# Remaining-row products of the feed-forward layer moved beside attention, with Silu built from Exp

## The chip, the cores and the metric

The kernel runs on one core of a Trainium2 chip, in fp32. The metric is device time in microseconds; the engines are TensorE (PE; its weight loads are PEld), VectorE (DVE), ScalarE (ACT), GpSimd (POOL) and SyncE (SP), whose queue issues most DMAs.

## The reference

One transformer block with modulation by a condition vector c, for x of 2 batches x 1024 tokens x 1024 features (`attn`, `ffn` abridged):

```python
mod = (silu(c) @ wmod).reshape(2, 6, 1, -1)          # sa, ca, ga, sb, cb, gb
h = layernorm(x) * (1 + ca) + sa
q, k, v = split(clip(h @ Wqkv.T, -8, 8))              # q, k: LayerNorm over 1024
scores = q k^T * 32**-0.5 + slope * (key - query)     # 32 heads of 32, causal
x = x + ga * (softmax(scores) @ v) @ Wout.T           # ga bounded away from 0
h = layernorm(x) * (1 + cb) + sb
act = silu((h @ Wg.T) * ag) * ((h @ Wu.T) * au)       # 2752 inner rows
x = x + gb * ((act @ Wd.T) * ad)
```

## The kernel before, in words

**Products.** Large products use a scheme of seven block products in place of eight (`seven`, the list `SEVEN`): a token block of 256 and a 1024-wide weight are split in 2 x 2 blocks, sums of blocks (A11, S1, ..., T1, ...) are multiplied, and the partial products P1, P2, U2, P5, U3, P53, U6 gather in two PSUM banks (`banks.pair()`). A partial product kept for later (P1, U2, P5) is copied out by ScalarE, its mate is added by VectorE.

**The inner rows.** Of the 2752 inner rows of the feed-forward layer, 2560 are handled in five groups by such products in the late stages. The last 192 (`REST`: 128 and 64 rows, here the *remaining rows*) are multiplied plainly: for each batch b and token block j (four of 256 tokens each) three *pieces* of eight matmuls, 128x256, over K = 1024: gate of 128 rows, up of 128 rows, and gate and up of 64 rows in one. Silu of the gate times the up goes to `rest_dram` for the down product.

**Stages in order.** (1) Modulation and projections of batch 0. (2) Attention of both batches: `attention` yields after each piece of work of a *unit* (four heads, one key block of 128), and `together` lays a generator of dense work, `dense_work`, between: projections of batch 1 while batch 0's attention runs, output products of batch 0 and of the first half of batch 1 while batch 1's runs. How much dense work is laid in by a given point follows from planned costs: `share(a)` with LEAD, DENSE0 and DENSE1, in planned us; a pair of 512-wide products counts 1.8. PE runs in exactly the order written (`pinned`); the other engines' and SP's order is set by a scheduler. (3) A stage of its own: the output products of batch 1's blocks j = 2, 3, all remaining-row products, and `second_batch`, which forms differences of the two batches' h2. (4) Gate and up products (gx, gy, ux, uy), with POOL forming weight sums. (5) Down products.

**A unit of attention.** Scores of four heads (two PSUM tiles sc0, sc1, one buffer each), Exp on ScalarE into p, a causal select on POOL, two units later the product with v (av), and sums of p on VectorE or POOL (`adders`). At the end of a group `settle` sums p over keys (`ones`) through a *turn bank* and stores it; after a group of 512 queries `reciprocals` loads the sums, inverts them and stores them.

**The output of one block**, `output`: `operand` loads the reciprocals (`rb`, four broadcasting DMAs) and ao, multiplies them and forms A11, A12, A21, A22, S1, S2, S4. 28 products follow; `read` adds mates, multiplies by the gate ga and adds to the residual rows xr. x1 is stored, rows are normalized to xn (`normalize`: bn_stats on VectorE, Ln and Exp on ScalarE, a correction on VectorE), and four transposes per block with scale and shift to h2 (`turned`, into h2t) are put on a list, `Todo`. `Todo.run` takes from this list between the products of the next block, each entry with the next turn bank (`banks.turn()`). In batch 1's attention there is a single turn bank, shared with `settle`.

**Buffers.** xr has four, A21 and A22 two each, A11, A12 and the S sums one. The remaining rows' weights are loaded after attention on ScalarE's queue, into memory of the attention pools; h2 blocks come back from memory by `fetch` (hl). Four PSUM banks (rps) hold their results.

Of the kernel before, what the change touches and what calls it, by code (L numbers as in the profile page):

```python
# [12 lines left out]
FP = mybir.dt.float32  # L13
AF = mybir.ActivationFunctionType
ALU = mybir.AluOpType
# [465 lines left out]
def kernel(  # L481
# [262 lines left out]
    def matmul(*args, **kw_):  # L744
        return in_order(nc.tensor.matmul(*args, **kw_))  # L745
# [112 lines left out]
    class Todo:  # L858
# [8 lines left out]
        def run(self, n, all_=False):  # L867
            for _ in range(min(n, len(self.list))):
                if not all_ and not self.banks.fresh():
                    return  # L870
                self.list.pop(0)(self.banks.turn())
                yield TURN

        def places(self, q0, n, side=lambda e: None):

# [337 lines left out]
    def operand(b, j, ap_):  # L1213

        qb, y0 = 2 * j * P // QB, 2 * j * P % QB
        rb = ap_.tile([P, KC, 2 * P], FP, tag="rb", name=f"rb_{b}_{j}")
        for g in range(4):
            nc.sync.dma_start(
                rb[ts(g, HD)],
                rec_dram[b][qb].rearrange("(k g) q -> g k q", g=4)[g][:, ds(y0, 2 * P)].partition_broadcast(HD),  # L1220
            )
        a = {
            q: ap_.tile(
                [P, KC // 2, P], FP, tag=q, name=f"ao{q}_{b}_{j}",
                bufs=2 if q in ("A21", "A22") else None,
            )
            for q in ("A11", "A12", "A21", "A22", "S1", "S2", "S4")
        }
        for m, kh, q, eng in (
            (0, 0, "A11", nc.vector), (0, 1, "A12", nc.gpsimd), (1, 1, "A22", nc.vector), (1, 0, "A21", nc.gpsimd),  # L1230
        ):
            nc.sync.dma_start(a[q], ao_dram[b][qb][:, ds(kh * 4, 4), ds(y0 + m * P, P)])
            eng.tensor_mul(a[q], a[q], rb[:, ds(kh * 4, 4), ts(m, P)])
        nc.vector.tensor_add(a["S1"], a["A21"], a["A22"])
        nc.vector.tensor_sub(a["S2"], a["S1"], a["A11"])
        a["S3"] = a["A21"]
        nc.gpsimd.tensor_sub(a["S3"], a["A11"], a["A21"])
        nc.gpsimd.tensor_sub(a["S4"], a["A12"], a["S2"])
        return a

    gates = {}

    def output(b, js, pools, banks, bt, todo, keep, made={}, q0=1):

        gap_, ap_, tkp, partp, hbp, sm = pools
        while (b, 2 * js[0] * P // QB) not in settled:
# [6 lines left out]
        for j in js:  # L1253
# [11 lines left out]
            def read(q, bank):  # L1265
                if q in ("P1", "U2", "P5"):
                    part_t[q] = partp.tile([P, 512], FP, tag=q, name=f"o{q}_{b}_{j}")
                    nc.scalar.copy(part_t[q], bank)
                    return
                m, n = QUAD[q]  # L1270
                yg = partp.tile([P, 512], FP, tag=f"yg{n}", name=f"yg_{q}_{b}_{j}")
                if q == "U6":
                    nc.vector.tensor_mul(yg, ga[:, ts(n, HALF)], bank)
                else:
                    nc.vector.tensor_add(yg, part_t[MATE[q]], bank)
                    nc.gpsimd.tensor_mul(yg, yg, ga[:, ts(n, HALF)])
                nc.gpsimd.tensor_add(xs[m][:, ts(n, HALF)], xs[m][:, ts(n, HALF)], yg)

# [10 lines left out]
            for m in range(2):  # L1289
                for g in range(2):  # L1290
                    def go(bank, m=m, g=g, xn=xn, h2=h2, j=j):
                        turned(
                            xn[m], bank, lambda k: h2[:, k, m, :],
                            lambda k: modt[:, 4, k, b : b + 1], lambda k: modt[:, 3, k, b : b + 1], g, False,
                        )
                        if (m, g) == (1, 1):
                            nc.sync.dma_start(h2_dram[b][j], h2)
                            if b == 0:
                                inner_b("B11", h2[:, 0 : KC // 2], j, hbp, nc.vector)
                                inner_b("B21", h2[:, KC // 2 :], j, hbp, nc.vector)  # L1300
                    todo.add(go)

    def second_batch(j, pool, h0, h1):

# [16 lines left out]


    OUT_US = 112.0
    LEAD, DENSE0, DENSE1 = 16.0, 370.0, 136.0

    def halves(half, jb):
        return (nc.vector, nc.gpsimd)[half]
# [14 lines left out]
            eng.dma_start(dst, src_[:, ds(r, n)].rearrange("(k p) f -> p k f", p=P))  # L1342
        return w

    def rest_rows(pairs, rest_w, pool, psp, tiles):

        n1 = REST[1][1]
        ib = 4 * NSB
        for b, j in pairs:
            hl = tiles[b, j].rearrange("p k h t -> p k (h t)")  # L1350
            ps = []
            for r in range(3):
                bank = psp.tile([P, 512], FP, tag="rp", name=f"rest_{b}_{j}_{r}")[:, 0:256]
                for k in range(KC):
                    matmul(bank, rest_w[r][:, k, :], hl[:, k, :], start=(k == 0), stop=(k == KC - 1))
                ps.append(bank)
                yield 3.4
            sg = pool.tile([P, 2, 256], FP, tag="rsg", name=f"rsg_{b}_{j}")
            ac = pool.tile([P, 2, 256], FP, tag="rac", name=f"rac_{b}_{j}")
            nc.scalar.activation(sg[:, 0], ps[0], AF.Silu, scale=vt[:, R_AG + ib : R_AG + ib + 1])  # L1360
            nc.scalar.activation(
                sg[64 : 64 + n1, 1], ps[2][0:n1], AF.Silu, scale=vt[0:n1, R_AG + ib + 1 : R_AG + ib + 2]
            )
            nc.vector.scalar_tensor_tensor(
                ac[:, 0], ps[1], vt[:, R_AU + ib : R_AU + ib + 1], sg[:, 0], ALU.mult, ALU.mult
            )
            nc.vector.scalar_tensor_tensor(
                ac[64 : 64 + n1, 1], ps[2][64 : 64 + n1],
                vt[64 : 64 + n1, R_AU + ib + 1 : R_AU + ib + 2], sg[64 : 64 + n1, 1], ALU.mult, ALU.mult,
            )  # L1370
            nc.sync.dma_start(rest_dram[0][:, b, j], ac[:, 0].rearrange("p (h t) -> p h t", h=2))
            nc.sync.dma_start(
                rest_dram[1][0:n1, b, j], ac[64 : 64 + n1, 1].rearrange("p (h t) -> p h t", h=2)
            )

    def in_range(pool, psp):

# [90 lines left out]
    def dense_work():  # L1468
        yield from dense0
        with tc.tile_pool(name="wdsum", bufs=2) as dwp:  # L1470
            steps = itertools.chain.from_iterable(down_weights(i, dwp) for i in range(4 * NSB))

            def side(n, e):
                at = 7 * n + e
                if at % 2 == 0 and at >= 2:
                    next(steps, None)

            yield from projections(1, qpools, banks, 1, side=side)
            for _ in steps:
                pass  # L1480
        early.close()
        hbp = right["hb"] = ost.enter_context(tc.tile_pool(name="hb", bufs=1))
        wop = ost.enter_context(tc.tile_pool(name="wo", bufs=1))
        gap_, tkp, partp, osm, aop = [
            ost.enter_context(tc.tile_pool(name=n, bufs=k))
            for n, k in (("oga", 1), ("tok", 4), ("opart", 1), ("osmall", 2), ("ao", 1))
        ]
        opools = (gap_, aop, tkp, partp, hbp, osm)
        made = {(0, 0): operand(0, 0, opools[1])}
        bt = weights_b(wop, wout_t, "o", wt_dram[3])  # L1490
        out_args.extend((opools, banks, bt, Todo(banks), keep))
        yield from output(0, range(NJ), *out_args, made)
        yield from output(1, range(NJ // 2), *out_args)

# [10 lines left out]

    together(attention(apools, (halves, mostly), banks), dense_work(), share)
    att.close()
    opools, _, bt, todo, _ = out_args
    pair_st = ctx.enter_context(ExitStack())
    rest_st = ctx.enter_context(ExitStack())  # L1510
    pair_pool = right["rest"] = pair_st.enter_context(tc.tile_pool(name="pair", bufs=1, side="right"))
    rest_pool = rest_st.enter_context(tc.tile_pool(name="rest", bufs=1, side="right"))
    rps = rest_st.enter_context(tc.tile_pool(name="rest_ps", bufs=4, space=PSUM))

    def fetch(b, j, eng=nc.sync):
        kept[b, j] = pair_pool.tile(
# [1 line left out]
        )  # L1518
        eng.dma_start(kept[b, j], h2_dram[b][j])

    def rows(*pairs):
        return rest_rows(pairs, rest_w, rest_pool, rps, kept)

    def second(j):
        for go in sum(second_batch(j, pair_pool, kept[0, j], kept[1, j]), []):
# [1 line left out]

    def with_turns(rows_):

        together(rows_, todo.run(len(todo.list), True), lambda a: 0.16 * (a - 9.0))  # L1530

    fetch(0, 0, nc.scalar)
    rest_w = rest_weights(rest_pool, nc.scalar)
    fetch(1, 0, nc.scalar)
    made = {(1, NJ // 2): operand(1, NJ // 2, opools[1])}
    fetch(0, 1)
    with_turns(rows((0, 0), (1, 0)))
    fetch(1, 1)

    def between():  # L1540
        yield from rows((0, 1))
        second(0)
        yield from rows((1, 1))

    together(
        between(), output(1, range(NJ // 2, NJ), *out_args, made, 3), lambda a: 0.6 * OUT_US / 2 * a / 20.6
    )
    in_range(rest_pool, rps)
    fetch(0, 2)
    second(1)  # L1550
    fetch(0, 3)
    with_turns(rows((0, 2), (1, 2)))
    second(2)
    alone(rows((0, 3), (1, 3)))
    ost.close()
    late_pools.close()
    pinned[0] = False
# [438 lines left out]
```

## Time and profile before

| | us |
|---|---|
| median of 3 runs (lowest, highest) | 2951.07 (2949.82, 2956.16) |
| the profiled execution | 2953.39 |
| its span, first to last instruction | 2951.7 |
| mean granted TensorE clock, share of full speed | 0.971 |

One profiled execution gives all lines of this document. In a timeline row the columns are start, duration, engine, source line, operation, output and input, shape and count, and in brackets the idle time before it and what ended it. A group row gives minimum, median and maximum in ns. A row of stages gives for each engine its busy time and, in brackets, its instructions. A fp32 matmul is two instructions in the trace.

### The profile page before, as it was taken

To read this page: it belongs to the slowest core of one execution; us is meant where nothing else is said; L and a number is where in the kernel's file an instruction comes from. 1 tells how busy PE (TensorE), PEld (TensorE's weight loads), DVE (VectorE), ACT (ScalarE), POOL (GpSimd) and SP (SyncE) were. 2 spreads that over 40 slices of the span, in tenths; PEclk is the share of its full clock that TensorE was granted. 3 is DMA by queue.
4 is the path that set the end of the run, shared out by engine and by line. 5 is a ranking of instruction groups with operands and counts; after the bars stand their busy time and mean duration, and the time that the engine had idled before them with its cause. 6 is when DMAs were issued, how large, how long until landed. Compare 5 with 4: busy or idle time off the path is not lost. (4 is left out here: it accounts for less than half of the span.)

```text
span 2951.7 us, 29883 instructions
## 1 busy us (share of the span) xinstructions
PE 2733.9 (93%) x10271; PEld 1338.6 (45%) x10271; DVE 1434.9 (49%) x2285; ACT 686.6 (23%) x1523; POOL 1289.9 (44%) x1270
## 2 busy tenths in 40 slices
PE   6999897899999898878798999999999998999998
PEld 2444332333333232222465444444444446888776
DVE  5666522456553454655554344453535445434442
ACT  1222232354434455555111011010101100000000
POOL 3312145524363665556357346463644641222343
PEclk9999998999999889999899999999999999999999
DMA  8777787462652644432676758575765759554542
GB/s 335 296 256 283 295 287 229 140 221 92 221 164 69 216 151 144 148 106 85 184 239 216 245 174 283 162 269 178 243 213 176 245 156 283 162 157 135 164 146 80
DMA packets 377571, 579.12 MB, mean 196 GB/s; under 512 B 21590, under 2 KB 278712, under 8 KB 366276
## 3 DMA queue, kind: packets, MB, share of 16 engines
q1 hardware_dynamic: 359768, 554.54, 58.0%
q10 hardware_dynamic: 17644, 22.59, 2.5%
q8 instruction: 84, 1.38, 0.2%
q14 instruction: 75, 0.61, 0.1%
HBM read 411.89 MB, written 165.17 MB: 196 GB/s over the span
## 5 line engine op out<-in xcount | busy, mean ns | idle before, releaser
L1056 ACT ACTIVATE p<-sc,kw 128x128 f32<-128x128 f32 (+3 forms) x1024 | 422.2, 514 | 353.9 <-PE sc L745 340.7
L745 PE MATMUL bank<-wT,a 128*128 128x512 f32 x768 | 364.7, 619 | 14.0 <-DVE raw L951 7.1
L1088 POOL TENSOR_TENSOR p<-p,p 128x1024 f32<-128x1024 f32 (+3 forms) x128 | 264.1, 2064 | 236.5 <-PE av L745 209.3
L1088 DVE TENSOR_TENSOR p<-p,p 128x1024 f32<-128x1024 f32 (+3 forms) x192 | 239.7, 1261 | 187.9 <-POOL p L1060 141.4
L745 PE MATMUL bank<-wB,a 128*128 128x512 f32 x576 | 264.3, 603 | 3.2 <-DVE raw L951 1.9
L745 PE MATMUL sc<-cq,ck 32*128 32x512 f32 (+3 forms) x1536 | 196.3, 553 | 69.9 <-ACT p L1056 69.7
L745 PEld LDWEIGHTS bank<-wT,a 128*128 128x128 f32 x768 | 144.0, 197 | 202.6 <-issue 183.9
L1060 POOL TENSOR_SCALAR_AFFINE_SELECT p<-p 128x256 f32<-128x256 f32 x256 | 135.6, 543 | 148.1 <-ACT p L1056 146.0
L745 PE MATMUL av<-p,cv 128*32 128x512 f32 (+3 forms) x1536 | 174.0, 517 | 19.2 <-POOL p L1060 19.2
L745 PEld LDWEIGHTS bank<-wB,a 128*128 128x128 f32 x576 | 104.6, 190 | 149.1 <-issue 129.7
L745 PEld LDWEIGHTS sc<-cq,ck 32*128 32x128 f32 x1536 | 66.1, 190 | 201.3 <-ACT p L1056 121.2
L1781 PE MATMUL gy<-bt,sig 128*128 128x512 f32 x280 | 133.5, 599 | 12.2 <-DMA bt<-bop_B 8.3
L1781 PE MATMUL uy<-bt,siu 128*128 128x512 f32 x280 | 132.2, 594 | 0.0
L1781 PE MATMUL ux<-bt,siu 128*128 128x512 f32 x280 | 131.6, 592 | 0.0
L1781 PE MATMUL gx<-bt,sig 128*128 128x512 f32 x280 | 131.6, 592 | 0.0
L745 PEld LDWEIGHTS av<-p,cv 128*32 128x32 f32 x1536 | 33.8, 110 | 137.4 <-issue 85.5
L951 DVE TENSOR_TENSOR raw<-P,bank 128x512 f32<-128x512 f32 x48 | 32.9, 685 | 126.8 <-PE bank L745 117.5
L1781 PEld LDWEIGHTS gy<-bt,sig 128*128 128x128 f32 x280 | 52.6, 190 | 82.5 <-issue 74.1
L1781 PEld LDWEIGHTS uy<-bt,siu 128*128 128x128 f32 x280 | 53.6, 192 | 67.8 <-issue 66.6
L1781 PEld LDWEIGHTS gx<-bt,sig 128*128 128x128 f32 x280 | 53.2, 190 | 67.0 <-issue 66.6
L1781 PEld LDWEIGHTS ux<-bt,siu 128*128 128x128 f32 x280 | 53.2, 190 | 67.0 <-issue 65.1
L745 PE MATMUL rest<-hl,restw 128*128 128x256 f32 x288 | 67.7, 394 | 14.9 <-DMA restw<-in_L_ffn_Wu_dram 14.9
(416 smaller groups left out, 4510.7 us busy)
## 6 DMA issues: line engine op xcount, KB each, us to landing
bt<-bop_T SPq DMA_DIRECT2D x140, 512.0 KB
bt<-bop_B SPq DMA_DIRECT2D x99, 512.0 KB
a<-hop SPq DMA_DIRECT2D x20, 1792.0 KB
wm<-in_L_wmod_dram SPq DMA_DIRECT2D x48, 512.0 KB
wB<-in_L_attn_Wqkv_dram SPq DMA_DIRECT2D x21, 1024.0 KB
aq_S<-act_S SPq DMA_DIRECT2D x16, 1280.0 KB
qk<-qs SPq DMA_DIRECT2D x16, 1024.0 KB
act_S<-asS SPq DMA_DIRECT2D x30, 512.0 KB
```

The costliest lines, as they stand in the source:

```text
L745: return in_order(nc.tensor.matmul(*args, **kw_))
L951: nc.vector.tensor_add(dst, part_t[MATE[q]], bank)
L1056: nc.scalar.activation(p[:, g, lo:hi], sp[:, g, lo:hi], AF.Exp, bias=kw[:, d, h_ : h_ + 1])
L1060: nc.gpsimd.affine_select(out=p[:, :, 0:P], in_=p[:, :, 0:P], pattern=[[0, 2], [1, P]], compare_op=ALU.is_ge, fill=0.0, base=0, channel_mu ...
L1088: adders[b](half, jb).tensor_add(dst, dst, ps[half][:, :, 0:n])
L1781: nc.tensor.matmul(ps.rearrange("p (j t) -> p j t", j=NJ), ins[mat][qa][:, c2, :], bt[:, :, c2, :], start=(q in ("P1", "P2", "P5") and c2 ...
```

## The change

`rest_rows` becomes `rest_piece`: one piece is an entry of the `Todo` list, behind the four transposes of its block, and works on the block's h2 still on chip. So the pieces of batch 0 and of batch 1's blocks 0 and 1 are taken between output products. Blocks 2 and 3 of batch 1 stay after the output. The weights are loaded on SP's queue with the pools of the output stage; DENSE1 goes from 136 to 205 planned us. Silu(g) is formed as g / (1 + exp(-g)): Identity and Exp on ScalarE, then a minimum with an addition, a reciprocal and a product on VectorE. To make room xr gets two buffers, A21 and A22 one, and the gated partial sum is formed in place of its own tile. After attention the list is emptied, with two more turn banks, then the output of blocks 2 and 3 of batch 1 runs by itself.

```diff
-                self.list.pop(0)(self.banks.turn())
-                yield TURN
+                more = self.list.pop(0)(self.banks.turn())
+                if more is None:
+                    yield TURN
+                else:
+                    yield from more
...
-                bufs=2 if q in ("A21", "A22") else None,
...
-                yg = partp.tile([P, 512], FP, tag=f"yg{n}", name=f"yg_{q}_{b}_{j}")
                 if q == "U6":
+                    yg = partp.tile([P, 512], FP, tag="yg", name=f"yg_{q}_{b}_{j}")
                     nc.vector.tensor_mul(yg, ga[:, ts(n, HALF)], bank)
                 else:
-                    nc.vector.tensor_add(yg, part_t[MATE[q]], bank)
+                    yg = part_t[MATE[q]]
+                    nc.vector.tensor_add(yg, yg, bank)
...
+            if rest is not None:
+                for r in range(3):
+                    todo.add(rest_piece(b, j, r, *rest))
...
-    LEAD, DENSE0, DENSE1 = 16.0, 370.0, 136.0
+    LEAD, DENSE0, DENSE1 = 16.0, 370.0, 205.0
...
+    def rest_piece(b, j, r, rest_w, pool):
...
+        def go(bank):
+            hl = kept[b, j].rearrange("p k h t -> p k (h t)")
+            ps = bank[:, 0:256]
+            for k in range(KC):
+                matmul(ps, rest_w[r][:, k, :], hl[:, k, :], start=(k == 0), stop=(k == KC - 1))
+            if r != 1:
+
+                g, e = tile_("rg", r), tile_("re", r)
+                nc.scalar.activation(g[hi], ps[lo], AF.Identity, scale=ag_)
+                nc.scalar.activation(e[hi], g[hi], AF.Exp, scale=-1.0)
+                nc.vector.tensor_scalar(e[hi], e[hi], FAR, 1.0, ALU.min, ALU.add)
+                nc.vector.reciprocal(e[hi], e[hi])
+                nc.vector.tensor_mul(g[hi], g[hi], e[hi])
+                sig[b, j, gate] = g
+            if r != 0:
+                ac = tile_("rac", r)
+                nc.vector.scalar_tensor_tensor(ac[hi], ps[hi], au_, sig[b, j, gate][hi], ALU.mult, ALU.mult)
+                nc.sync.dma_start(
...
+            yield 3.5
...
-            for n, k in (("oga", 1), ("tok", 4), ("opart", 1), ("osmall", 2), ("ao", 1))
+            for n, k in (("oga", 1), ("tok", 2), ("opart", 1), ("osmall", 2), ("ao", 1))
         ]
+        rwp = ost.enter_context(tc.tile_pool(name="restw", bufs=1))
...
-    rps = rest_st.enter_context(tc.tile_pool(name="rest_ps", bufs=4, space=PSUM))
+    rps = rest_st.enter_context(tc.tile_pool(name="rest_ps", bufs=2, space=PSUM))
...
-        together(rows_, todo.run(len(todo.list), True), lambda a: 0.16 * (a - 9.0))
-
-    fetch(0, 0, nc.scalar)
-    rest_w = rest_weights(rest_pool, nc.scalar)
-    fetch(1, 0, nc.scalar)
+        together(rows_, todo.run(len(todo.list), True), lambda a: 0.3 * (a - 3.0))
+
+    banks.others = banks.others + [rps.tile([P, 512], FP, tag=f"rq{i}", name=f"rq{i}", bufs=1) for i in range(2)]
     made = {(1, NJ // 2): operand(1, NJ // 2, opools[1])}
+    fetch(0, 0)
+    fetch(1, 0)
+    alone(todo.run(len(todo.list), True))
     fetch(0, 1)
-    with_turns(rows((0, 0), (1, 0)))
     fetch(1, 1)
-
-    def between():
-        yield from rows((0, 1))
-        second(0)
-        yield from rows((1, 1))
-
-    together(
-        between(), output(1, range(NJ // 2, NJ), *out_args, made, 3), lambda a: 0.6 * OUT_US / 2 * a / 20.6
-    )
+    second(0)
+    alone(output(1, range(NJ // 2, NJ), *out_args[:-1], None, made, 3))
     in_range(rest_pool, rps)
+    second(1)
     fetch(0, 2)
-    second(1)
     fetch(0, 3)
-    with_turns(rows((0, 2), (1, 2)))
+    with_turns(rows(2))
     second(2)
-    alone(rows((0, 3), (1, 3)))
+    alone(rows(3))
```

More of the change, by code (lines that the diff above doesn't have):

```diff
@@ L1241, with output @@
     gates = {}
-    def output(b, js, pools, banks, bt, todo, keep, made={}, q0=1):
+    def output(b, js, pools, banks, bt, todo, keep, rest=None, made={}, q0=1):
         gap_, ap_, tkp, partp, hbp, sm = pools
@@ L1343, in rest_weights @@
         return w
-    def rest_rows(pairs, rest_w, pool, psp, tiles):
+    def rest_piece(b, j, r, rest_w, pool):
         n1 = REST[1][1]
         ib = 4 * NSB
[L1349 to L1362, printed above, removed]
-            )
[L1364 to L1374, printed above, removed]
@@ new lines, in rest_piece, with tile_ @@
+        gate, lo = (0, slice(0, P)) if r < 2 else (1, slice(0, n1))
+        hi = slice(64, 64 + n1) if gate else lo
+        ag_, au_ = (vt[rows_, R_ + ib + gate : R_ + ib + gate + 1] for rows_, R_ in ((lo, R_AG), (hi, R_AU)))
+        def tile_(nm, r):
+            return pool.tile([P, 256], FP, tag=nm, name=f"{nm}_{b}_{j}_{r}")
+        def go(bank):
[15 more added lines that the diff above has]
+                nc.sync.dma_start(
+                    rest_dram[gate][0 : n1 if gate else P, b, j], ac[hi].rearrange("p (h t) -> p h t", h=2)
+                )
+            yield 3.5
@@ L1376, in in_range @@
+        return go
+    sig = {}
     def in_range(pool, psp):
@@ L1490, in dense_work @@
         bt = weights_b(wop, wout_t, "o", wt_dram[3])
-        out_args.extend((opools, banks, bt, Todo(banks), keep))
+        rest = rest_weights(rwp, nc.sync), rwp
+        out_args.extend((opools, banks, bt, Todo(banks), keep, rest))
         yield from output(0, range(NJ), *out_args, made)
@@ L1507 @@
     att.close()
-    opools, _, bt, todo, _ = out_args
+    opools, _, bt, todo, _, rest = out_args
     pair_st = ctx.enter_context(ExitStack())
@@ L1519, in fetch, with rows @@
         eng.dma_start(kept[b, j], h2_dram[b][j])
-    def rows(*pairs):
-        return rest_rows(pairs, rest_w, rest_pool, rps, kept)
+    def rows(j):
+        for r in range(3):
+            yield from rest_piece(1, j, r, *rest)(rps.tile([P, 512], FP, tag="rp", name=f"rest_{j}_{r}"))
     def second(j):
@@ L1528, in with_turns @@
     def with_turns(rows_):
-        together(rows_, todo.run(len(todo.list), True), lambda a: 0.16 * (a - 9.0))
-    fetch(0, 0, nc.scalar)
-    rest_w = rest_weights(rest_pool, nc.scalar)
-    fetch(1, 0, nc.scalar)
+        together(rows_, todo.run(len(todo.list), True), lambda a: 0.3 * (a - 3.0))
+    banks.others = banks.others + [rps.tile([P, 512], FP, tag=f"rq{i}", name=f"rq{i}", bufs=1) for i in range(2)]
     made = {(1, NJ // 2): operand(1, NJ // 2, opools[1])}
+    fetch(0, 0)
+    fetch(1, 0)
+    alone(todo.run(len(todo.list), True))
     fetch(0, 1)
-    with_turns(rows((0, 0), (1, 0)))
     fetch(1, 1)
-    def between():
-        yield from rows((0, 1))
-        second(0)
-        yield from rows((1, 1))
-    together(
-        between(), output(1, range(NJ // 2, NJ), *out_args, made, 3), lambda a: 0.6 * OUT_US / 2 * a / 20.6
-    )
+    second(0)
+    alone(output(1, range(NJ // 2, NJ), *out_args[:-1], None, made, 3))
     in_range(rest_pool, rps)
+    second(1)
     fetch(0, 2)
-    second(1)
     fetch(0, 3)
-    with_turns(rows((0, 2), (1, 2)))
+    with_turns(rows(2))
     second(2)
-    alone(rows((0, 3), (1, 3)))
+    alone(rows(3))
     ost.close()
```

## The prediction

> **What bounds the kernel now.** I read the page's busy line first, then the stages, since one share over 2951.7 us says little. TensorE (PE) is busy 93%, so time comes only from stretches where it waits, or from work laid into them. The profile in stages:
>
> ```profile
> PE 2733.9 (93%) x10271; PEld 1338.6 (45%) x10271; DVE 1434.9 (49%) x2285; ACT 686.6 (23%) x1523; POOL 1289.9 (44%) x1270
> ```
> ```profile
> core 0: us, PE busy (x) PEld busy (x) DVE busy (x) ACT busy (x) POOL busy (x), PEclk, DMA share, GB/s
> 390.00:990.00 600.00, 555.69 (x2522) 204.68 (x2520) 279.43 (x431) 238.96 (x559) 281.42 (x279) 0.96 0.55 185
> 990.00:1412.00 422.00, 350.09 (x2033) 113.14 (x2032) 231.92 (x344) 228.78 (x553) 244.31 (x232) 0.92 0.40 124
> 1412.00:1586.00 174.00, 153.53 (x580) 106.74 (x579) 93.85 (x178) 22.82 (x36) 75.66 (x67) 0.95 0.76 236
> 1586.00:1650.00 64.00, 54.57 (x120) 23.43 (x119) 27.09 (x34) 7.92 (x12) 49.25 (x67) 0.92 0.67 214
> ```
>
> The second row is attention of batch 0 with the projections beside it, the third attention of batch 1 with the output products. The fourth is the stage between attention and the gate and up products, which holds all the remaining-row products. Batch 1's attention leaves PE 72 us idle (422 - 350), the stage after it 20 (174 - 153.5). The waits of 990 to 1412 say why:
>
> ```profile
> ACT p L1056 <- PE sc L745: 130.0, 80, 6.5
> PE sc L745 <- ACT p L1056: 55.1, 43, 7.1
> DVE st_f L716 <- POOL xr L1277: 50.7, 19, 4.8
> ACT lv_f L721 <- DVE mv_f L717: 28.5, 4, 8.9
> ```
>
> PE and ScalarE wait for each other in turn: scores must be through Exp before the next scores may enter their bank. What one unit (four heads, one key block) takes with and without other work shows in PE's timeline, batch 0 first, then batch 1:
>
> ```profile
> 943.99 1.14 PE L745 MATMUL sc<-cq,ck 32*128 32x512 f32 x8
> 945.06 3.70 PE L745 MATMUL bank<-wB,a 128*128 128x512 f32 x8
> 948.69 0.43 PE L745 MATMUL av<-p,cv 128*32 128x128 f32 x8
> 949.04 1.14 PE L745 MATMUL sc<-cq,ck 32*128 32x512 f32 x8
> ```
> ```profile
> 1221.94 1.14 PE L745 MATMUL sc<-cq,ck 32*128 32x512 f32 x8
> 1223.02 1.06 PE L745 MATMUL av<-p,cv 128*32 128x512 f32 x8
> 1225.63 0.71 PE L745 MATMUL sc<-cq,ck 32*128 32x512 f32 x4 [1.55 <-ACT p L1056]
> ```
>
> Four dense 512-wide products (3.44 us) in a unit make 5.05 us, no wait left; an empty unit takes 3.69. So such a lump is only partly free.
>
> The end of the chain of waits lies in the gate, up and down products, unchanged. What counts is when the first gx starts (1585.98) and whether it is then fed.
>
> **The skill.** "Perfetto Trace Analysis", Optimization Strategy, advises interleaving regimes with different limits; agreed in principle, the 72 us are there. "VectorE: DVE Perf Modes", First, the fixed hardware budget, says that a reciprocal repeats a divide step eight times; the trace agrees (946 ns for 128x128 against 280 ns for a maximum or minimum of that size). "ScalarE: Activation LUTs", What ACT_TABLE_LOAD costs, gives 1283 ns for a load; the page's groups show eight of 1283 ns in the stage after attention, the Silu and Ln/Exp sets in turn. "TensorE: Matmul & The Clock Gate", What's actually happening, says PE's clock halves after an idle window of about 3.4 us; agreed below.
>
> ```profile
> 1439.83 12.41 PE L745 MATMUL rest<-hl,restw 128*128 128x256 f32 x48 [14.92 <-DMA restw<-in_L_ffn_Wu_dram]
> 1540.55 10.53 PE L745 MATMUL rest<-hl,restw 128*128 128x256 f32 x48
> ```
>
> The same 24 products (two instructions each) take 12.41 us after a pause, 10.53 warm. A **piece** of eight is thus 3.44 us (start to start 10.3 / 3); 24 pieces, 82.6 us, all lie after attention now.
>
> **Part by part.** I take positions from the built order of instructions.
>
> 1. *Pieces moved.* 15 of the 24 now stand before the last scores: four pairs of batch 0 and the first of batch 1. 51.6 us of PE work enters attention. With DENSE1 at 205, the rest of output (1,1), 14 products of 0.86 us, and its transposes enter as well: 12.5 us. Together 64.
>
> What 64 us costs there: (a) by the lumps. In 512-wide units 5.27 us (median of batch 0's units with 3.44 us dense) against 3.7 empty: +1.6; where pairs of output products share the unit, about +3; in 384-, 256- and 128-wide units (3.1, 2.4 and 1.8 empty) +2.2 to +3.1. Over the 15 places in the built order (seven wide and empty, four shared, four narrow) 11 + 12 + 11 = 34 us; the 14 products and the pairs pushed into other units about 10. Sum **+44**. (b) by the two batches as they are: batch 0 holds 351 us of dense work in 600 us, batch 1 122 in 422: (600 - 422) / (351 - 122) = 0.78 per us, 50 for 64. Part of that is other work, so I take 44; bounds 22 (each lump absorbing a 2 us wait) and 64 (none).
>
> 2. *Silu from Exp.* Each moved pair has two sigmoids: Identity and Exp on ScalarE (0.47 each by the rsg row, 1.9 per pair against 0.95 plus table loads), then on VectorE minimum-and-add (0.33, nearest rows 0.34 to 0.41), reciprocal 128x256 (unseen; 946 ns for half the width, so 1.9, bounds 0.95 and 1.9), product (0.41): 2.6 each, 5.3 per pair, 26 us on VectorE in attention, which is 55% busy there. Behind the minimum, which waits for Exp, stand the sums of p and h2t in VectorE's order; behind the Identity stand the next Exps of attention. The third piece keeps the only turn bank until sigmoid and product are through. What a held bank costs shows here:
>
> ```profile
> 1147.56 1.12 PE L748 MATMUL bank<-ident,xn 128*128 128x128 f32 x4 [7.59 <-DVE h2t L851]
> ```
>
> Five such holds and one more normalize in attention (ScalarE's Ln waiting on bn_aggr, 28.5 us over four now): I take **+10** (0 to 35). The eight table loads go (10 us of ScalarE): PE worked on remaining-row products and output products meanwhile, 0.
>
> 3. *Fewer buffers.* xr from four to two: SP, in order, now waits for j's normalize and store before it loads j+1's rows, and chunk loads, ao and sum stores queue behind. A chunk is fetched a group ahead (16 to 30 us), a store takes 4 to 6: inside the +10. yg in place costs nothing: each partial sum has one reader. A21 and A22 single: see below. Weights earlier: 1.5 MB at a DMA share of 0.55, no one waits; their 14.9 us wait after attention goes.
>
> 4. *The stage after attention*, from T, the end of the last sums of p (1412.2 before). Before: 174. After, by the built order: four transposes and h2t, 16 x 0.34, to T+6; three pieces to T+17. Then PE waits for the operand of (1,2). This was ready at T+36 already:
>
> ```profile
> 1448.23 2.50 POOL L1233 TENSOR_TENSOR aoA<-aoA,rb 128x512 f32<-128x512 f32 x2 [12.59 <-DMA rb<-rec]
> ```
>
> Its chain (sums, store, load, reciprocal, store, four rb loads) gains from a less crowded DMA, loses some 4 us because the reciprocal rc now stands behind h2t, sigmoid and a second_batch difference on VectorE: T+36 again, 19 us of PE idle that the remaining rows filled before. 28 products of 0.86, 24 us, plus 2 cold: T+62. Then the price of the single buffers: (1,3)'s four aoA loads stand on SP behind the x stores of (1,2), which wait for POOL's last sum (2.5), load (3 to 4), VectorE multiplies after normalize: 8.5 idle, T+70. 24 + 2 transposes + 1 cold: T+97. One piece, then 6 idle until normalize of (1,3) is through, as it was 10.5 after the last product before (1540.4 to 1550.9): T+106. Two pieces, transposes and h2t mixed with a sigmoid: T+117, one piece, gx at T+121, two more pieces (7) between the first gx: **128 against 174, -46**, bounds -36 and -58.
>
> 5. *Gate and up start.* Its 9.4 us of PE idle (64 - 54.6) hang on POOL's sums and bop stores. second_batch now waits for no remaining-row product, but has less cover: 0, bounds -6 and +6.
>
> Sum 44 + 10 - 46 = **+8**; on the execution of 2953.4 (span 2951.7 and 1.7 around it) 2961; the runs' median lies 2.3 lower, so **2960**, with rounding.
>
> **Rivals.** *Attention swallows it* (0.30): the 72 us of idle really take lumps, VectorE has 45% free. Then +25 there and -50 after: 2926. For it: idle exceeds the added 64; denser PE keeps its clock (0.92 now). Against: batch 0, already filled with such lumps, shows 5.27 us a unit. It decides if the lumps average under 1.2 us. *In-order stalls* (0.20): the held bank and VectorE's waits cost 3 us at each of the ten sigmoids: attention +75, after -40: 2986. For it the 7.59 line; against, only five third pieces hold long. *It doesn't do what it says*: the built order shows the 15 pieces in attention; no chance given.
>
> **Numbers.** The forecast's case has 0.50, own range 2945 to 2975; of it 0.03 faster, 0.13 same, 0.34 slower. The first rival gives 0.27 faster and 0.03 same, the second 0.20 slower. 0.2% (6 us) is about what a measurement can tell from no change. Faster 0.30, same 0.16, slower 0.54; 2922 to 2994 leaves out the outer parts of both rivals.
>
> **What would show it.** Batch 1's attention near 476 us, gx some 128 after its end (counting the two late pieces), units with a piece near 5.3 us, an idle of 15 to 20 us waiting for rb and one of 8 between the two outputs, no table load before the gate stage. Wrong if attention grows under 30 us, or the stage after it takes over 145.

## The result and the profile after

The changed kernel takes 2981.67 us (median of four runs, 2979.58 to 2989.66), the kernel before 2953.48 beside it (four runs, the three of the table above among them): ratio 1.0097, 95% interval 1.0074 to 1.012. It is **slower by about 28 us**. The forecast was 2960, with a range of 2945 to 2975 for its own case and of 2922 to 2994 with the rivals. The profiled execution of the changed kernel is the slowest of its four, 2989.66 us with a span of 2987.9; its distance to the span before, 36.2 us, is thus 8 us more than that of the medians.

The busy line and three stages, batch 1's attention in the first row, the stage behind it in the second, the start of the gate and up products in the third:

```profile
PE 2750.3 (92%) x10271; PEld 1339.7 (45%) x10271; DVE 1487.8 (50%) x2333; ACT 684.2 (23%) x1532; POOL 1289.8 (43%) x1270
```
```profile
990.00:1478.30 488.30, 422.61 (x2352) 162.94 (x2350) 290.87 (x409) 242.12 (x585) 259.03 (x245) 0.94 0.39 118
1478.30:1607.30 129.00, 86.95 (x276) 51.44 (x274) 83.87 (x157) 7.95 (x18) 66.86 (x57) 0.86 0.83 265
1607.30:1671.00 63.70, 55.39 (x137) 26.42 (x135) 27.97 (x36) 7.53 (x13) 50.41 (x65) 0.95 0.70 232
```

PE's count of instructions is the same. Attention ends 66 us later (1478.3 against 1412.2), the stage behind it is 45 us shorter (129 against 174) but has twice the idle time, 42 us (129 - 87) against 20. Cut at four points that every PE timeline has (last scores of batch 0, first output product, last sums of p, first gx, first dx), the way from the one profile to the other is:

| stretch | before | after | difference |
|---|---|---|---|
| last scores of batch 0, start | 955.7 | 954.2 | -1.5 |
| from there to the first output product | 5.3 | 16.9 | +11.6 |
| from there to the last sums of p ("attention") | 451.2 | 507.2 | +56.0 |
| from there to the first gx ("stage") | 173.7 | 129.0 | -44.7 |
| first gx to first dx | 869.8 | 886.4 | +16.6 |

That is +38.0; the rest of the kernel gives 1.7 back. A unit with a piece, in PE's timeline:

```profile
1085.11 1.14 PE L745 MATMUL sc<-cq,ck 32*128 32x512 f32 x8
1086.18 0.64 PE L745 MATMUL av<-p,cv 128*32 128x256 f32 x8
1086.75 3.72 PE L745 MATMUL bank<-h2t,restw 128*128 128x256 f32 x16
1090.40 0.93 PE L745 MATMUL sc<-cq,ck 32*128 32x384 f32 x8
```

Scores to scores, 5.29 us: the length that the units of batch 0 foretold. Eleven of the 15 units with a piece hold no other dense work; they take 4.87 to 6.10 us, 5.29 in the median. The other four, with output products or sums of p beside the piece, take 7.6 to 11.6. The waits of attention:

```profile
ACT p L1059 <- PE sc L745: 160.1, 82, 8.0
PE sc L745 <- ACT p L1059: 40.9, 28, 4.4
```

PE's waits for Exp fell from 55.1 to 40.9 us, only 14 us. Others came in their place: in all, from the first output product on, PE is idle 65.7 us of attention (507.2 - 441.5 busy) where it was idle 72.0. PE's busy time there rose by 62 us (379.3 to 441.5; the prediction had counted 64). So **62 us of work entered attention and took away 6 us of waiting**.

Behind attention the waits are open:

```profile
1506.93 9.04 PE L745 MATMUL bank<-wB_o,aoA 128*128 128x512 f32 x16 [13.82 <-DVE aoA L1235]
...
1533.11 3.70 PE L745 MATMUL bank<-wT_o,aoA 128*128 128x512 f32 x8 [3.41 <-DVE oP L1279]
1547.50 9.23 PE L745 MATMUL bank<-wB_o,aoA 128*128 128x512 f32 x16 [10.69 <-DVE aoA L1235]
...
1588.63 1.11 PE L748 MATMUL bank<-ident,xn 128*128 128x128 f32 x4 [9.41 <-DVE xn L730]
...
1606.32 1.21 PE L745 MATMUL rest<-h2t,restw 128*128 128x256 f32 x2 [3.48 <-DVE h2t L851]
...
1613.99 7.14 PE L745 MATMUL rest<-h2t,restw 128*128 128x256 f32 x32 [1.85 <-DVE rac L1380]
```

The three long ones are for the operand of block 2, the operand of block 3 and the normalize of block 3. Remaining-row pieces stood there before. The last line shows two pieces that still run behind the first gx (1607.33).

### The profile page after: what moved, and what is told of

The parts are those of the page before. It is cut to its first block, busy times and chain, and to the rows that moved or that the text cites. A ratio compares the mean times of both kernels' runs of the same rounds, so it can differ in the third digit from the quotient of the medians.

```text
span 2987.9 us, 29929 instructions
## 1 busy us (share of the span) xinstructions
PE 2750.3 (92%) x10271; PEld 1339.7 (45%) x10271; DVE 1487.8 (50%) x2333; ACT 684.2 (23%) x1532; POOL 1289.8 (43%) x1270
## 4 chain that ended last, share of the span: by engine, by line
PE 44%; issue 4%; DVE 4%; DMA 4%; POOL 4%; ACT 1%; SPq 0%; POOLq 0%; DVEq 0%; ACTq 0%
PE gx L1791 7%; PE ux L1791 7%; PE dx L1904 7%; PE gy L1791 6%; PE uy L1791 6%; PE dy L1904 5%; PE bank L745 3%; PE sc L745 1%; DMA bt<-bop_B 1%; PE av L745 1%; ACT p L1059 1%; DMA bop_T<-inner_T 1%; POOL xr L1281 1%; DVE p L1091 1%; DVE asS L1745 0%
## 5 line engine op out<-in xcount | busy, mean ns | idle before, releaser
L1091 DVE TENSOR_TENSOR p<-p,p 128x1024 f32<-128x1024 f32 (+3 forms) x192 | 248.4, 1306 | 186.2 <-POOL p L1063 149.6
L1791 PE MATMUL gy<-bt,sig 128*128 128x512 f32 x280 | 137.0, 613 | 16.6 <-DMA bt<-bop_B 10.1
L745 PE MATMUL bank<-wB_o,aoA 128*128 128x512 f32 x128 | 70.8, 691 | 40.3 <-DVE aoA L1235 24.5
```

Of the source, the lines that this page charges most:

```text
L1091: adders[b](half, jb).tensor_add(dst, dst, ps[half][:, :, 0:n])
L1791: nc.tensor.matmul(ps.rearrange("p (j t) -> p j t", j=NJ), ins[mat][qa][:, c2, :], bt[:, :, c2, :], start=(q in ("P1", "P2", "P5") and c2 ...
```

## The experiments

The theory at the outset: attention pays for TensorE's pieces, lump by lump. The rivals: in-order stalls from the sigmoid and the held turn bank, and the buffers. The table gives each run's ratio to the kernel before (run on the same chip beside it) and, from its one profile, four of the stretches above. PE idle is the sum of the idle times in brackets in PE's timeline, from the wait ahead of the first output product to 220 us behind the first gx. The first expectations count attention from another point (478.6 us for the changed kernel, where the table has 507.2), so compare their differences.

| kernel | ratio, 95% interval | to first output product | attention | stage | gx to dx | PE idle |
|---|---|---|---|---|---|---|
| before | 1 | 5.3 | 451.2 | 173.7 | 869.8 | 108 |
| after | 1.0097 (1.0074 to 1.012) | 16.9 | 507.2 | 129.0 | 886.4 | 135 |
| e1_pool_order | 1.0082 (1.0063 to 1.0101) | 8.1 | 510.9 | 129.0 | 883.8 | 128 |
| e2_fewer_buffers | 1.0019 (1.001 to 1.0027) | 16.7 | 450.8 | 175.5 | 873.5 | 122 |
| e3_no_sigmoid | 1.0099 (1.0077 to 1.012) | 16.5 | 512.4 | 140.4 | 874.5 | 137 |
| e4_one_of_eight | 1.0057 (1.0039 to 1.0076) | 16.2 | 483.9 | 129.4 | 893.4 | 176 |
| e6_weights_early | 0.9959 (0.9943 to 0.9975) | 8.2 | 452.5 | 157.5 | 873.6 | 97 |
| e7_halves | 1.0116 (1.0096 to 1.0136) | 8.4 | 509.8 | 145.2 | 876.2 | 132 |
| e8_batch1_after | 1.0174 (1.0158 to 1.0189) | 8.4 | 521.0 | 149.0 | 884.3 | 145 |
| e9_dense136 | 1.0237 (1.0219 to 1.0254) | 8.1 | 468.8 | 212.7 | 879.2 | 156 |
| e10_six_in_attention | 0.9938 (0.9925 to 0.995) | 8.4 | 456.7 | 150.2 | 867.0 | 93 |
| e11_exp_after | 1.0045 (1.0032 to 1.0058) | 8.5 | 449.5 | 171.0 | 884.5 | 115 |
| e12_batch1_after_195 | 1.0099 (1.0085 to 1.0114) | 10.3 | 499.2 | 140.7 | 893.1 | 137 |
| e13_products_earlier | 0.9949 (0.9938 to 0.9961) | 8.1 | 455.3 | 150.7 | 872.9 | 97 |

### The late first output product: e1_pool_order and e2_fewer_buffers

The forecast had nothing ahead of attention. The first output product of the changed kernel:

```profile
971.14 2.90 PE L745 MATMUL bank<-wB_o,aoA 128*128 128x512 f32 x3 [15.79 <-DVE aoS L1237]
```

SP's queue shows why: the loads of its operand, which stood at 837 (rb) and 850 us (aoA) before, are issued only now, and the weights queue behind them.

```profile
949.12 0.43 SPq L1221 DMA_DIRECT2D rb<-rec  x1
...
...
955.96 5.70 SPq L1234 DMA_DIRECT2D aoA<-ao  x4
961.75 3.85 SPq L806 DMA_DIRECT2D wB_o<-in_L_attn_Wout_dram  x2
```

In the built programs, rb of output (0,0) begins at byte 134,688 of each partition before, and at 124,448 after: 10,240 bytes lower, two xr tiles and one tile of the gated sum. There it overlaps the partial sums U2 and P5 of the last projection block, which VectorE reads until the end of the projections.

```diff
# e1: the changed kernel
-            for n, k in (("oga", 1), ("tok", 2), ("opart", 1), ("osmall", 2), ("ao", 1))
+            for n, k in (("oga", 1), ("tok", 2), ("opart", 1), ("osmall", 2))
         ]
         rwp = ost.enter_context(tc.tile_pool(name="restw", bufs=1))
+        aop = ost.enter_context(tc.tile_pool(name="ao", bufs=1))
# e2: the kernel before, with tok 2, A21 and A22 single, yg = part_t[MATE[q]]
```

> The changed kernel with one edit: the pool of the remaining rows' weights is placed below the pool of the attention operands instead of above it, so that the operand tiles rb and aoA of output (0,0) no longer lie on memory that the last projection's partial sums (U2, P5) still use. Theory 'placement': the first output product starts near 961 us again instead of 971 us, batch 1's attention (979 to 1478 there) keeps its 478 us, the stage after it its 129 us; total about 10 us below the changed kernel, 2972. Rival 'crowded queue' (the late start comes from SP's order and the early weight loads, wherever the tiles lie): first product again near 971, total 2982 as the changed kernel.

> The kernel before with the change's buffers alone: xr two instead of four, A21 and A22 single, the product's partial sum scaled in its own tile; no remaining row is moved and Silu stays. Theory: rb of output (0,0) lies at the same address as in the changed kernel, so the first output product is about 10 us late (971 instead of 961); batch 1's attention stays within 5 us of 422, the stage after it between 174 and 182 (operand of (1,3) late); total +10 to +18, 2963 to 2971. Rival 'buffers cost nothing': 2953. Rival 'xr is what stalls attention': attention 432 or more and total above 2975.

The first output product in e1:

```profile
961.43 6.24 PE L745 MATMUL bank<-wB_o,aoA 128*128 128x512 f32 x8 [6.99 <-DMA wB_o<-in_L_attn_Wout_dram]
```

With the pools swapped it starts at 961.43 again (961.05 in the kernel before); with the buffers alone it is late, 16.7 us behind the last scores as in the changed kernel, while attention (450.8) and the stage (175.5) keep their length. Placement is thus shown as the cause of the late start. e2 as a whole is 0.1 to 0.27% slower than the kernel before, 3 to 8 us, which is of that size. xr and the single A21 and A22 cost attention nothing in e2; beside the pieces this was not tried. The 10 us that e1 was expected to gain on the whole did not show: its median, 2981.11, and that of the changed kernel can't be told apart (their intervals overlap), and in its profile attention is 3.7 us longer.

### What attention pays for: e3_no_sigmoid, e4_one_of_eight, e7_halves

```diff
# e3: the changed kernel (e is no longer made)
...
-                nc.scalar.activation(e[hi], g[hi], AF.Exp, scale=-1.0)
-                nc.vector.tensor_scalar(e[hi], e[hi], FAR, 1.0, ALU.min, ALU.add)
-                nc.vector.reciprocal(e[hi], e[hi])
-                nc.vector.tensor_mul(g[hi], g[hi], e[hi])
# e4: the changed kernel
-            for k in range(KC):
-                matmul(ps, rest_w[r][:, k, :], hl[:, k, :], start=(k == 0), stop=(k == KC - 1))
+            matmul(ps, rest_w[r][:, 0, :], hl[:, 0, :], start=True, stop=True)
# e7: e1, and each piece twice, for h = 0 and 1
...
-            return pool.tile([P, 256], ...)
+            return pool.tile([P, P], ...)
...
-                matmul(ps, rest_w[r][:, k, :], hl[:, k, :], ...)
+                matmul(ps, rest_w[r][:, k, :], hl[:, k, h, :], ...)
...
-            yield 3.5
+            yield 1.75
```

> The changed kernel without the sigmoid of the remaining rows: the gate is only scaled (Identity), and Exp, minimum-and-add, reciprocal and product are left out; all products stay. Theory 'lumps' (attention pays for TensorE's pieces): attention 470 to 475 instead of 478.6, stage after it 125 to 129, total 2972 to 2980. Rival 'in-order stalls' (Exp and reciprocal in front of the sums of p and the held turn bank): attention 455 or less, total below 2960.

> The changed kernel with one of the eight products (k = 0) of each piece of the remaining rows: seven eighths of their sum are left out; sigmoid, loads and stores stay. 15 x 3.0 = 45 us of TensorE work less in attention, 9 x 3.0 = 27 less after it. Theory 'lumps': attention 438 to 445 instead of 478.6, the stage after it and the start of the gate products some 15 to 20 less (its waits for the operands fill up what goes), total 2920 to 2930. Rival 'in-order stalls': attention stays at 460 or more, total above 2945.

> The changed kernel with the pools in the other order, and each piece cut in two halves of 128 columns with a turn of its own (1.7 us instead of 3.4), so twice as many turns and twice as many small instructions of the sigmoid. Theory 'the lump is larger than the hole' (a wait for Exp is 1.3 us on average, a piece 3.4): more holes are filled, waits for Exp fall from 42 us to 30 or less, first output product to last sums 495 to 503 instead of 510.9, total 2966 to 2974. Rival 'turns and chains': the holes lie where a turn is not allowed or the held bank costs as much; attention stays at 508 or more, total 2980 or more.

Neither theory alone holds. Without the sigmoid, VectorE is busy 29 us less in attention (265.7 against 294.7), and attention is no shorter (512.4 against 507.2). With 45 us less of TensorE work it is 23 us shorter, half of it. Where the other half went: PE idles 10.5 us more (76.0 against 65.5: waits for Exp 46.9 against 40.9, for rac 6.3 against 2.1), and its other instructions, the same in number, take 11 us longer, at a granted clock of 0.91 against 0.93. How the small steps and the pieces hang together shows at the first pieces of pair (0,1). VectorE and PE in the changed kernel, and then the same place in e4:

```profile
1162.28 1.22 DVE L1091 TENSOR_TENSOR p<-p,p 128x1024 f32<-128x1024 f32 x1
1163.41 1.74 DVE L1375 RECIPROCAL re<-re 128x256 f32<-128x256 f32 x1
1165.07 1.72 DVE L1091 TENSOR_TENSOR p<-p,p 128x1024 f32<-128x1024 f32 x1
1166.72 0.41 DVE L1376 TENSOR_TENSOR rg<-rg,re 128x256 f32<-128x256 f32 x1
1167.05 2.35 DVE L1091 TENSOR_TENSOR p<-p,p 128x1024 f32<-128x1024 f32 x2
1169.32 0.47 DVE L1380 SCALAR_TENSOR_TENSOR rac<-bank,vt,rg 128x256 f32<-128x256 f32 x1
```
```profile
1164.89 3.62 PE L745 MATMUL bank<-h2t,restw 128*128 128x256 f32 x16
1169.85 1.06 PE L745 MATMUL bank<-p,ones 128*32 128x512 f32 x8 [1.34 <-DVE rac L1380]
```
```profile
1158.59 0.59 PE L745 MATMUL bank<-h2t,restw 128*128 128x256 f32 x2
1165.51 1.93 PE L745 MATMUL bank<-p,ones 128*32 128x512 f32 x8 [6.32 <-DVE rac L1379]
```

Each small step of the sigmoid stands behind a sum of p in VectorE's order. The bank of the second piece (up) is read by the product into rac, which needs the sigmoid of the first; the next `ones` needs that bank. In the changed kernel the piece of 3.62 us covers most of this chain and 1.34 us are left open; with the piece cut to 0.59 us, 6.32 are. **Here lump and chain run side by side**: with the lump gone, the chain shows. This is one place of 5 us; no run takes lump and chain away together, so that the two overlap all over attention is not shown. Halves fit the holes better (waits for Exp 31.1 us against 41.9 in e1), but twice as many turns bring twice as many chains: PE's waits for rac are 20.2 us against 2.1, and attention stays at 509.8, as the rival had it.

e4 tells of the stage, too. Ahead of the first gx, 21 us of PE's work are missing (87.0 busy, now 65.9), and the stage is as long as ever. Its row (start and end, length, PE busy first):

```profile
1454.20:1583.60 129.40, 65.93 (x175) 32.65 (x176) 88.24 (x156) 7.83 (x18) 63.86 (x52) 0.75 0.82 254
```

The wait for the first operand has grown from 13.8 to 22.1 us, for the second from 10.7 to 15.3, for xn from 9.4 to 14.5; one of 7.4 us, for which the profile names no cause, stands ahead of the first gx. So in the changed kernel this stage is bound by the chain operand, products, normalize, operand, and not by PE. Any piece that attention took out of it left a hole.

### Pieces back behind attention: e8_batch1_after, e12_batch1_after_195, e9_dense136

```diff
# e8: e1, rest=None for batch 1, fetch(1, 0) ahead of fetch(0, 0)
# e12: the same with 195.0
-    LEAD, DENSE0, DENSE1 = 16.0, 370.0, 205.0
+    LEAD, DENSE0, DENSE1 = 16.0, 370.0, 184.0
...
     alone(todo.run(len(todo.list), True))
+    alone(rows(0))
...
-    alone(output(1, range(NJ // 2, NJ), *out_args[:-1], None, made, 3))
+    alone(output(1, [NJ // 2], *out_args[:-1], None, made, 3))
+    alone(rows(1))
+    alone(output(1, [NJ // 2 + 1], *out_args[:-1], None, {}, 3))
# e9: e1 with
+    LEAD, DENSE0, DENSE1 = 16.0, 370.0, 136.0
```

> The changed kernel with the pools in the other order, and the six pieces of batch 1's first half taken out of attention's turns (DENSE1 184) and laid into the two waits for the operands after it: three ahead of output (1,2), three between (1,2) and (1,3). Theory 'open waits behind attention': first output product to last sums 495 to 500 instead of 510.9, the stage after it 129 to 136 although 21 us of products are added to it, total 2965 to 2972. Rival 'the stage is as long as its products': stage 145 to 152, total 2978 to 2985.

> The run with batch 1's six pieces behind attention again, with DENSE1 195 instead of 184, so that attention holds the same output products as in the changed kernel and only the pieces leave it. Theory 'open waits behind attention': attention 503 to 506 from the first output product (510.9 with the three pieces), the stage after it 129 to 138, since the waits of 14.5 and 10.8 us for aoA take the 20.6 us; total 2972 to 2982. Rival 'the stage is as long as its products': 149, total 2992 or more.

> The changed kernel with the pools in the other order and DENSE1 back at 136: some 60 us of products and pieces fall out of attention to the stage after it, where one wait of 14 us can take them. Theory 'attention charges 0.8 us per us of work': attention 48 us shorter (463 from the first output product), stage 129 + 46 = 175, total 2979 to 2984, no gain. Rival 'attention charges 0.5 to 0.6' (as the run with one product of eight showed): attention 475 to 480, total 2990 to 2996. Rival 'attention charges all of it': attention 450, total 2966 to 2970.

Of the six pieces, the three of block 1 stood behind attention in e1 already, so three are added to the stage, 10.3 us, and not the 20.6 of the expectations. e8 and e9 went against all that was expected of them. e8's attention is 10 us longer than e1's with three pieces and some seven output products less in it; PE idles 83 us there against 67 (8.52 us in one wait for the sum of a group, rs, and 6.91 in one for h2t), and its clock is 0.90 against 0.93. Why is not shown. e12, with attention's products as in e1, is what e8 should have been: attention 499.2, 11.7 less for three pieces less, and the stage 140.7, 11.7 more for three pieces more. The waits for the two operands are shorter (13.3 us in the place of 14.5, 6.0 in the place of 10.8), but counted from the last sums of p the operands come 3.3 and 12.0 us later than in e1: the chain itself moved. Behind gx 9.3 us more appear (one wait of 12.5 us for POOL's wgS), and the ratio, 1.0099, is no better than e1's. The theory of open waits, to be filled by three pieces each, fell; with three pieces in the place of six, the rival's figure would be 139 us for the stage, and it came near (140.7). e9 has in attention the amount of work of the kernel before, with 31 us of pieces in the place of 27 us of output products, and takes 468.8 us, 16 more than e6 (below). Some 17 products of output (1,0) and all 28 of (1,1) now stand behind attention, with two normalizes and their transposes, and the stage is 84 us longer than e1's: 75 us of it is PE's busy time (163.2 against 88.0), 8 are idle. So attention gave back 42 us for what cost the stage 84. Pieces must not push products back into a stage that the products' chain bounds.

### What the stage gives without any move: e6_weights_early, e11_exp_after, e13_products_earlier, e10_six_in_attention

```diff
# e6: the kernel before, with e2's buffers, restw below ao as in e1, and
+        right["restw"] = rest_weights(rwp, nc.sync)
...
-    rest_w = rest_weights(rest_pool, nc.scalar)
+    rest_w = right["restw"]
# e11: e6, in rest_rows Identity, Exp, min/add, reciprocal, product for each
-            nc.scalar.activation(sg[:, 0], ps[0], AF.Silu, scale=...)
# e13: e6 with
-    LEAD, DENSE0, DENSE1 = 16.0, 370.0, 136.0
+    LEAD, DENSE0, DENSE1 = 16.0, 370.0, 150.0
# e10: e6 with rest_piece for pairs (0,2) and (0,3), and DENSE1 157.0
-        yield from output(0, range(NJ), *out_args, made)
+        yield from output(0, range(NJ // 2), *out_args, made)
+        yield from output(0, range(NJ // 2, NJ), *out_args, rest=(right["restw"], rwp))
...
-    with_turns(rows((0, 2), (1, 2)))
+    with_turns(rows((1, 2)))
...
-    alone(rows((0, 3), (1, 3)))
+    alone(rows((1, 3)))
```

> The kernel before, with three parts of the change: its buffers, the remaining rows' weights loaded early into a pool of the output stage (placed below the attention operands, as in the run with the pools in the other order), and no other move: all remaining rows stay behind attention, with Silu. Theory 'idle behind attention is what counts': the wait of 14.9 us for restw goes, everything else stays: first output product near 961, attention to its last sums 451 us from there, the stage to the first gx 158 to 164 instead of 173.7, total 2940 to 2947. Rival 'next in line': PE then waits for hl, the copy of h2t fetched after attention, or for the next operand, and the stage keeps 170 or more: 2952 to 2957.

> The kernel with the weights early and all remaining rows behind attention, with the sigmoid from Exp (Identity, Exp, minimum-and-add, reciprocal, product) in the place of Silu; nothing else. Theory 'the function costs nothing either way': eight table loads of 1.28 us go from ScalarE, some 42 us of small instructions come to VectorE, both beside TensorE: stage 155 to 161 as with Silu (157.5), total 2942 to 2950. Rival 'VectorE is the next limit behind attention' (88 us busy of 157 there, then 130): normalize and h2t come later, stage 165 or more, total above 2953. Rival 'table loads mattered': stage 150 or less, total below 2940.

> The kernel with the weights early and all remaining rows behind attention, with DENSE1 150 instead of 136: not pieces but the last 14 products of output (1,1) and its normalize move into attention. Theory: attention +9 to +12 (452 becomes 461 to 464), and behind it PE waits for hl, whose copy these products covered, so the stage falls by only 5 to 12: total 2943 to 2953. Rival 'output products cost attention more than pieces' (they share VectorE's and GpSimd's sums and a normalize): attention +15 or more, total above 2955. Rival 'attention has room for products': attention +5 or less, total below 2940.

> The kernel with the weights early and all remaining rows behind attention (2945.7 us in its run), with six of the 24 pieces moved into attention's turns in the changed kernel's form (pairs (0,2) and (0,3), DENSE1 157). Theory 'only filler is lost': attention charges 0.7 us per us, 14 us for 20.6, so 452 becomes 467; the stage after it falls by the 20.6 less what opens behind it, since these pieces cover normalize and second_batch of (1,3): 157 becomes 145 to 150; total 2950 to 2955, slower than without the move. Rival 'a filled stage gives all of it back': stage 137, total 2938 to 2942. Rival 'held bank and in-order waits': attention 475 or more, total above 2958.

**e6** takes the one wait that cost something, restw's 14.9 us, and moves no work: attention 452.5, stage 157.5 with 6.8 us idle, 2945.7 us, ratio 0.9959. The rival fell: where PE had waited, hl was there. The row of the stage, and the place in PE's timeline:

```profile
1417.20:1574.70 157.50, 150.72 (x578) 103.90 (x579) 88.72 (x178) 22.91 (x36) 75.37 (x66) 1.00 0.81 260
...
1426.25 3.60 PE L745 MATMUL bank<-wT_o,aoA 128*128 128x512 f32 x8
1429.68 10.52 PE L745 MATMUL rest<-hl,restw 128*128 128x256 f32 x48
```

**e11** went with its first rival, not with the theory: the sigmoid from Exp, put behind attention, costs 24 us (2969.9 against 2945.7), in the profiles 13.5 in the stage and 10.9 behind the first gx. VectorE is busy 126 us of the stage against 89. The largest wait, behind the first gx (1585.96), VectorE and PE:

```profile
1607.08 0.98 DVE L1167 TENSOR_TENSOR inner_T<-hl 128x256 f32<-128x256 f32 x1 [21.60 <-DMA bop_T<-inner_T]
...
1608.82 1.75 DVE L1366 RECIPROCAL rex<-rex 128x256 f32<-128x256 f32 x1
...
1616.82 0.69 DVE L1600 TENSOR_TENSOR gX<-g_P,gy 128x512 f32<-128x512 f32 x1
```
```profile
1617.56 3.78 PE L1788 MATMUL gy<-bt,sig 128*128 128x512 f32 x4 [21.14 <-DVE gX L1600]
```

A difference of `second_batch` waits for the store of its buffer, the two sigmoids of a pair stand behind it in VectorE's order, gX (a sum of partial products of the gate) behind the sigmoids, and PE behind gX. Of PE's 21.14 us some 11 are the end of the wait for the store, the other 10 the steps between it and gX. With Silu the rows have only the product into rac on VectorE, and in e6 PE waits 0.4 us for this gX.

**e13** bore its theory for the stage (6.8 us shorter, PE waiting 7.75 us for hl) and the last rival for attention, which took the 14 products for 2.8 us; the total, 2940.2, lies between what the two expected. **e10** came out faster where the theory had slower: six pieces, 20.6 us of work, cost attention 4.2 us where 14 were expected.

```profile
966.00:1422.70 456.70, 396.97 (x2241) 138.78 (x2241) 260.18 (x369) 241.21 (x580) 263.05 (x246) 0.92 0.43 134
1422.70:1572.90 150.20, 133.78 (x483) 88.50 (x482) 90.51 (x175) 21.07 (x32) 80.02 (x72) 0.95 0.85 269
```

Idle in attention fell by 11 us against e6 (59.7 against 70.8), and PE's busy time rose by 15 us (381.7 to 397.0), less than the pieces' 20.6. The stage got back only 7.3 of the 20.6 us, since normalize (5.95 us) and transposes of block 3 then stood open. Against the kernel before: 2937.4 us, ratio **0.9938** (0.9925 to 0.995), the lowest of all and faster than both kernels. Its interval overlaps those of e6 and e13, so a gain of the six moved pieces over e6 is not clear of the noise; of the 8.4 us between the two profiles 6.6 lie behind the first gx, and why is open.

## Why the prediction was right, and where not

**Right.** The sign; the unit of 5.3 us with a piece (5.29 in the median of those without other dense work); the three places of the waits behind attention (19, 8.5 and 6 us foretold, 13.8, 10.7 and 9.4 measured, the sums alike: 33.5 and 33.9); no table load in attention or behind it until 1647.5 us, when the gate products run. The cold starts came too: the first 16 instructions of the outputs of blocks 2 and 3, after 13.8 and 10.7 us of idle, took 9.04 and 9.23 us where 16 warm ones took 7.03, as "TensorE: Matmul & The Clock Gate", What's actually happening, says of an idle window.

**Right in sum, not in its parts.** Attention was to grow by 54 us and grew by 56.0 from the first output product on (by 66 from 990 us on, the prediction's own window, since that product came late). Step 1 put +44 on lumps, step 2 +10 on stalls. Taken away alone, seven eighths of the pieces' products gave back 23 us, and the sigmoid none: neither term came as it was put, and that their sum fits is luck in part. Nor is there a price per us: e10's first 20.6 us cost 4.2, the changed kernel's 64 cost 58 (e1 against e6, both with the pools in one order). The rival "attention swallows it" holds for most of the six pieces and not for fifteen with the products of output (1,1).

**Right by luck.** The measured 2981.67 lies above the 2945 to 2975 of the prediction's own case; it is in the full range only because the rival "in-order stalls" (2986) was given room. By the total this rival is the nearer one, but attention grew by 56 and not by 75, and without the sigmoid it did not shrink (e3). The stage, -44.7 where -46 was foretold, agrees by chance as well: step 4 put the first gx at 121 us behind the last sums of p and counted 7 us of late pieces on top; the first gx came at 129, and the pieces still followed.

**Wrong, three steps of the sum.**

- Step 3, fewer buffers, "inside the +10": it counted buffers, not addresses. Smaller pools shift what is placed behind them; the first output product came 11.6 us later.
- Step 4, the first gx 8 us late: two waits, for oP and h2t (3.4 and 3.5 us), were not foreseen.
- Step 5, the start of gate and up, put at 0: besides 7 us of pieces, gx to dx grew by 9.6 us. Waits for rac, gX and gC grew by 1.8, 2.5 and 2.8 us, one of 1.5 has no named cause, those for bop_B shrank by 6.1, and the 1,959 gate and up instructions themselves took 6.8 us longer (854.9 against 848.1). Why they did is not shown.

From +8, the 11.6 us and some 18 of steps 4 and 5, with the 2 us of attention, less the 1.5 and 1.7 us that the ends gave back, make up the +36 of the profiled executions. The medians differ by 28.

Step 2 priced the sigmoid only where it stood in attention. With all eight pairs behind attention it costs 24 us (e11); with the three pairs that the changed kernel has there, leaving it out gained nothing (e3: stage and gx to dx together 1014.9 us against 1015.4).

**What is not settled.** Why fifteen pieces with 14 products cost so much more than six pieces. With seven eighths of the pieces' products gone, attention is still 31 us longer than e6's (e4), although the 14 products alone cost 2.8 (e13) and the sigmoid nothing. e9 and e8 say that it isn't the amount alone (equal or less work, 16 and 10 us more); whether it is the pairs (0,0) and (0,1), which all the dear versions and no cheap one have in attention, or the groups in which they fall, was not tried.

## What to carry to other kernels

Idle time of the bottleneck engine in one stage is not room: ask what ends each wait, and what the moved work itself makes wait; here 62 us of work used up 6 us of idle. Work on which little waits can be the filler of a stage bound by a chain: before moving it away, leave it out once and see whether the stage gets shorter (e4: not by 1 us). Putting it back elsewhere is not free either, since its small steps stand in other engines' orders (e11) and the chain can move with it (e12). After a change of buffers look where the pools behind them now lie, and whose memory their first loads wait for.

## What the runs showed of the hardware

- A reciprocal's time on VectorE went with its columns and not with its rows: 1.74 to 1.75 us both for 128x256 and for 64x256, and 946 ns for 128x128, where a product of 128x256 took 0.41. "VectorE: DVE Perf Modes", First, the fixed hardware budget, tells of a divide step that is repeated eight times, which fits the price beside a product; the sizes are the runs'.
- The granted clock of the stage behind attention fell as PE's idle time in it rose: 1.00 with 6.8 us idle (e6), 0.86 with 42 (the changed kernel) and 0.75 with 63 (e4).
- A wait passed from engine to engine by the order of instructions: VectorE's 21.6 us for one store delayed two sigmoids and a sum behind it that don't read that buffer, and PE, which needed the sum, waited 21.1 us, some 11 of them for that store (e11).
